# One core, three fused layers: a new order of loads, queries and attention work, and the moves of turned weights on two queues

## The chip, the core and the metric

The kernel runs on one core of one Trainium2 chip. Times are device microseconds (us) of one launch. A core has five engines with a queue of instructions each: TensorE (PE: matmuls and transposes, with its weight loads listed apart as PEld), VectorE (DVE), ScalarE (ACT), GpSimd (POOL) and SyncE (SP), which here only issues DMAs. ACT can issue DMAs too. Every engine works through its own queue in order. Matmuls write to PSUM, which the kernel uses as eight banks of 128 x 512 float32.

The metric is the median of three runs. The profiled execution is another one, with its own time.

## What is computed

Tokens are `x[16, 512, 256]`, all in float32. Three residual layers follow each other:

```python
x = x + 0.5 * slot_ffn(layernorm(x))
x = x + attention(layernorm(x))
x = x + 0.5 * slot_ffn(layernorm(x))

def attention(x):                         # 16 heads of 64, causal, rotary q and k
    q = rope(x @ Wq + bq); k = rope(x @ Wk + bk); v = x @ Wv + bv
    probs = softmax(where(causal, q @ k.T / 8, -inf))
    return (probs @ v) @ Wo + bo

def slot_ffn(x):                          # 16 slots, 16 experts of width 1024, heads of 16
    o = q0 + mha(q0, x, x, d_*)           # slots gather from the tokens
    h = layernorm(o) * g + b              # slot e goes to expert e
    o = o + (silu(h @ W1 + b1) * silu(h @ Wg + bg)) @ W2 + b2
    return mha(x, o, o, c_*)              # tokens read the slots
```

## The kernel before

**Stages.** `ffn(0)`, then `attention`, then `ffn(1)`. An ffn has three parts. `slots_and_experts` loops over the 16 batches i (with two more rounds for the tail): `width(b)` turns a normalized batch so that its width lies on the partitions (8 PE transposes, line 239), `slot_weights` scores the slots (p_ds, line 550), `slot_sums` adds up the tokens (p_z, line 586), `gathered` (p_mo, line 600) projects four batches at a time, `half_of_slots` (p_o, line 340, then its `turned`, p_oT) makes half of the slots ready for the experts. `experts` then goes through 16 experts; each reads three weight tiles of 1 MB that SP loads into twelve buffers, and a buffer is loaded again when its reader is done. `combine` is the third part (p_cs, p_vw, p_catT, p_cy).

**Queries.** The projection of a batch's tokens for `combine`, `queries(b)` (p_cq, line 383, 8 matmuls), can be put anywhere before `combine`. One is called in the slots' loop, two at its end (lines 501 and 503), two after it (lines 514 and 515), and the rest are `fillers` of `experts`: one per expert, and as many of the last experts get one as there are fillers.

**Order.** PE's order is written by hand for the whole kernel. In the slots' loop and in attention the orders of DVE, ACT, POOL and SP are the program's too; elsewhere (the first loads, `combine`) a planner chooses them.

**Attention.** A unit u is one batch and four heads: 64 units. Step u of the loop at line 1101 works on five units at once, as a pipeline:

- `sums(u)`: weights times values (p_av, line 1054, 32 matmuls on 128 rows x 64 columns of the array), and ACT's two writes of oT with the bias;
- of unit u+1 (`old`): the four `turn_most`, `turn_corner` and `turn_rest` (seven DVE transposes of 32 x 32 blocks into the tile sq, line 1001), POOL's scaling of the last quarter of the weights before them, then `move`: sixteen DMAs of 160 KB which carry blocks from 32 partitions q of sq to 32 partitions k of prT (line 1024, all on SP). sq and prT are single tiles. `sums(u+1)` waits for the sixteen;
- of unit u+2 (`new`): `scores` (p_as, line 956: four row tiles of 32 rows side by side) of token tile 3, later of tiles 2, 1 and 0; `exps` (DVE masks and takes the minimum out of PSUM, line 974, ACT takes the exponential, line 978); `scaled` (DVE's reciprocal, line 983, then POOL, line 986);
- of unit u+1: `values` (p_v, line 920, in two halves of 8 matmuls, ACT copies each);
- of unit u+3: queries and keys with rotary (p_q and p_k, line 898; DVE's eight products, line 904, and POOL's four sums, lines 909 and 910). At a new batch (`fresh`, every fourth unit) also `enter` (ACT normalizes), `width` (p_ahT, line 883) and `with_bias` (POOL);
- `leave(u, 0)` and `leave(u, 2)`: the output projection (p_ay, line 1070, 16 matmuls). Its addition to x on DVE (line 1076) is handed back as a function; the next step calls it after `move`.

In PE's order the step is: sums, scores of tile 3, half of the values, queries, keys, the other half of the values, the scores of tiles 2, 1 and 0, leave. Queries, keys, values, leave and `width` use the whole array (128 rows x 128 columns).

PSUM banks are taken in turn: a group takes the bank of the group eight places earlier, and waits until that one has been read. `token_stats` is a batch-norm pair on DVE (lines 198 and 199) that later layer norms need; `spread` and `scales` make the inverse deviations of two batches from them, through a square root on ACT.

**First loads.** SP issues the four pieces of x[0], then d_Wq and d_Wk, then the other x; ACT issues the slot query and three small rows. In `combine` of ffn 0, at j = 0 attention's weights are requested (`ahead[0]`) and at j = 9 `first_pieces` (`ahead[1]`) takes the statistics of batches 0 and 1 in one go (`pair_stats(0)`, 8 pairs) and starts attention.

Of the kernel before, what the change touches and what calls it, by code (L numbers as in the profile page):

```python
# [9 lines left out]
F32 = mybir.dt.float32  # L10
AF = mybir.ActivationFunctionType
ALU = mybir.AluOpType
# [3 lines left out]
P = 128  # L16
# [31 lines left out]
def macaron_kernel(ctx: ExitStack, tc: tile.TileContext, a: dict, out: bass.AP):  # L48
# [47 lines left out]


    with tc.tile_pool(name="setup", bufs=1) as su:
        for t in range(NT):
            nc.sync.dma_start(xs[0][:, t, :], xin[0][:, t, :])  # L100
        sq = su.tile([NS, D], F32, tag="sq", name="sq")
        nc.scalar.dma_start(sq, a["slot_query"][0])
        d_wq = chunks(su.tile([P, NC, D], F32, tag="d_wq", name="d_wq"), a["d_Wq"], nc.sync)
        d_wk = chunks(su.tile([P, NC, D], F32, tag="d_wk", name="d_wk"), a["d_Wk"], nc.sync)
        drow = su.tile([3 * NC, P], F32, tag="drow", name="drow")
        for r, nm in enumerate(("d_bq", "d_bk", "d_bv")):
            nc.scalar.dma_start(drow[r * NC:(r + 1) * NC, :], a[nm].rearrange("(c p) -> c p", p=P))
# [216 lines left out]
    def slots_and_experts(n, ss, load, w, for_slots, hTs, kT, vT):  # L324
# [70 lines left out]
        with tc.tile_pool(name=f"disp{n}", bufs=2) as dp, \  # L395
# [37 lines left out]
            with tc.manual_schedule(engines={mybir.EngineType.DVE, mybir.EngineType.Activation,  # L433
                                             mybir.EngineType.Pool, mybir.EngineType.SP}):
                for i in range(NB + 2):
# [7 lines left out]
                    count(1)  # L443
                    if i < NB:
                        at, scaled = slot_weights(dp, i, hTs[i], lambda: count(1))
                    ahead = i + 2 if i < 2 else i + 1 if i > 2 else NB
                    if ahead < NB:
                        width(ahead)
                    if i - 1 in back:
# [48 lines left out]
                    ahead = i + 3 if i < 1 else i + 2 if i > 1 else NB  # L498
                    if ahead < NB:
                        hs[ahead] = normalized(dp, ahead, 4)  # L500
                queries(order.pop(0))
                gathered(NB // GB - 1, zT, moT, wvm)
                queries(order.pop(0))
                tail = half_of_slots(1)
        gp.close()
        with tc.tile_pool(name=f"late{n}", bufs=1) as lw, \
# [202 lines left out]
    def combine(n, cp, qTs, kT, vT, c_wo, cbo, last, ahead, later):  # L709
# [82 lines left out]
        for j in range(nj + 4):  # L792
            b = j // 2
            if ahead is not None and j == 0:
                ahead[0]()
            if ahead is not None and j == 9:
                pieces = ahead[1]()
            if j < nj:
                weigh(j, kbd)
                if j % 2 == 0:  # L800
                    values(b, vbd)
                    if b + 1 < NB:
                        nxt = of_slots(b + 1)
                    fetch(b + 3)
                else:
                    kbd, vbd = nxt
            if j == 3:
                later()
            if 0 <= j - 3 < nj:
                turned(j - 3)  # L810
            if j >= 4:
                onto_tokens(j - 4)
            if j >= nj - 1:
                for one in pieces[:2]:
                    one()
                del pieces[:2]
# [27 lines left out]
    def attention(qp, wq, wk, wv, wo, cos, sin, row):  # L844
# [87 lines left out]
        class Weights:  # L932
# [82 lines left out]
                self.turn(1, (0, HG), [(1, 2)], 1, (1, 3))  # L1015
                self.turn(1, (0, HG), [], 0, (0,))

            def move(self):


                prT = prTs[self.u] = ap.tile([P, NSQ, HG, blocks * SQ], F32, tag="prT", name=f"prT{self.nm}")
                for k in range(NSQ):
                    for q in range(NSQ):
                        nc.sync.dma_start(prT[k * SQ:(k + 1) * SQ, q, :, :], self.sq[q * SQ:(q + 1) * SQ, k, :, :])

            def turn_at_once(self):

# [37 lines left out]
        def leave(u, t0):  # L1065
            b, hg = units[u]
            py = ps(f"p_ay{b}_{hg}_{t0}")
            for t in range(2):
                for pair in range(HG // 2):
                    nc.tensor.matmul(py[:, t * D:(t + 1) * D], oTs[u][:, pair, (t0 + t) * P:(t0 + t + 1) * P],  # L1070
                                     wo[:, hg * (HG // 2) + pair, :],
                                     start=(pair == 0), stop=(pair == HG // 2 - 1))

            def added():
                xt = xs[b][:, t0:t0 + 2, :]
                nc.vector.tensor_tensor(xt, py.rearrange("p (t d) -> p t d", t=2), xt, ALU.add)
                if hg == NHG - 1:
                    nc.sync.dma_start(xout[b][:, t0:t0 + 2, :], xt)
            return added

# [14 lines left out]
        seen = 2 * NHG  # L1097
        with tc.manual_schedule(engines={mybir.EngineType.DVE, mybir.EngineType.Activation,
                                         mybir.EngineType.Pool, mybir.EngineType.SP}):
            gone = []  # L1100
            for u in range(-2, nu):
                new = ws[u + 2] = Weights(u + 2) if u + 2 < nu else None
                qk = queries_keys(u + 3)
                old = ws.get(u + 1)
                fresh = u + 3 < nu and units[u + 3][1] == 0
                if fresh:
                    enter(units[u + 3][0])
                if u + 2 == nu:
# [6 lines left out]
                if old and u + 2 == nu:  # L1115
                    old.turn_at_once()
                elif old:
                    old.turn_most(0)
                    old.scaled((1, 0), slice(0, HG // 2))
                    old.turn_most(1)  # L1120
                    old.scaled((1, 0), slice(HG // 2, HG))
                    old.turn_most(2)
                    old.turn_most(3)
                    old.turn_corner()
                    old.turn_rest()
                    old.move()
                for one in gone:
                    one()
                if fresh:
                    with_bias(units[u + 3][0])  # L1130
                if u + 4 in stds:
                    scales((u + 4) // (PB * NHG), stds.pop(u + 4))
                if fresh:
                    width(units[u + 3][0])
                if new:
                    new.scores((3,))
                    new.exps((3,))

                for at in range(seen, min(u + 13, NB * NHG)):
                    token_stats(*divmod(at, NHG))  # L1140
                seen = max(seen, u + 13)
                if u >= NHG + 1:
                    token_stats(*divmod(u - NHG - 1, NHG))
                if new:
                    new.scaled((3,))
                if 0 <= u + 1 < nu - 1:
                    values(u + 1, 0)
                for one in qk:
                    one()
                if 0 <= u + 1 < nu - 1:  # L1150
                    values(u + 1, 2)
                if 0 <= u + 5 < nu and (u + 5) % (PB * NHG) == 0:
                    stds[u + 5] = spread((u + 5) // (PB * NHG))
                if new:
                    new.scores((2,))
                    new.scores((1, 0))
                    new.exps((2,))
                    new.exps((1, 0), lambda: new.scaled((2,)))

                if u == nu - NHG:  # L1160
                    for g in range(NB // PB - 1):
                        pair_rstd(g)
                if u == nu - 1:
                    for g in range(PB):
                        entered[g] = xs[g]
                        for t in range(NT):
                            i = (g % PB) * NT + t
                            nc.vector.tensor_scalar(xs[g][:, t, :], xs[g][:, t, :], mvs[g // PB][:, i, 0:1],
                                                    rstds[g // PB][:, i:i + 1], ALU.subtract, ALU.mult)
                gone = [leave(u, 0), leave(u, 2)] if u >= 0 else []  # L1170
                if u >= nu - 2:
                    for one in gone:
                        one()
                    gone = []
            token_stats(NB - 2, NT - 1)
        yield
    with ExitStack() as es:
# [3 lines left out]
            stage.append(attention_weights(es.enter_context(tc.tile_pool(name="attw", bufs=1, side="right"))))  # L1181

        def first_pieces():
            pair_stats(0)
            pair_rstd(0)
            stage.append(attention(es.enter_context(tc.tile_pool(name="attq", bufs=1, side="right")), *stage.pop()))
            return next(stage[0])

# [44 lines left out]
```

## Time and profile before

| What | us |
|---|---|
| median of three runs (2343.24 to 2343.98) | 2343.69 |
| the profiled execution's own time | 2343.35 |
| its span, first to last instruction | 2341.6 |
| PE busy | 2286.4 |
| DVE busy | 1754.4 |
| ACT busy | 1123.7 |
| POOL busy | 1062.1 |

The stages in the span: ffn 0 from 0 to about 417, attention to about 1953, ffn 1 to the end. The granted TensorE clock was 0.992 over the span.

A busy PE says little of how fast it works, since matmuls overlap in the array and their ends are modelled; the start of one group and the start of the next say more. In rows of the timeline the columns are start, duration, engine, line, operation and tiles; the number in brackets is idle time before the row and what ended it. Matmul rows carry the array's rows x columns (128*128, 32*128, 128*64). Rows of DMA-issuing instructions (SPq, ACTq) are not counted as busy.

### The profile page before, as it was taken

How to read it: one execution, taken by the hardware profiler on the slowest of the kernel's cores; microseconds unless marked ns; L12 is line 12 of the kernel's file. 1: busy time of each engine (PE TensorE's matmuls, PEld its weight loads, DVE VectorE, ACT ScalarE, POOL GpSimd, SP SyncE). 2: the span in 40 equal slices, each digit the busy share in tenths (PEclk: the TensorE clock that was granted, in tenths of full speed). 3: DMA queues.
4: the chain of work that ended last, by engine and by line, in shares of the span. 5: the costliest groups of instructions: out<-in, count | busy, mean ns of one | idle time of the engine just before them, and what ended most of it. 6: DMA issues, size and time to landing. Idle time of an engine off the chain costs nothing. (4 is left out here: it accounts for less than half of the span.)

```text
span 2341.6 us, 42264 instructions
## 1 busy us (share of the span) xinstructions
PE 2286.4 (98%) x14496; PEld 1454.2 (62%) x14496; DVE 1754.4 (75%) x4659; ACT 1123.7 (48%) x3047; POOL 1062.1 (45%) x1692
## 2 busy tenths in 40 slices
PE   7999999899999999999999999999999999998999
PEld 5664588465565656565656565656656566664588
DVE  6732388888888888888898888888888865432387
ACT  5742243445455545454545545554555454542233
POOL 2210053565555655555656555556565541210043
PEclk9999999999999999999999999999999999999999
DMA  7839851354545464545555555646464643739834
GB/s 231 242 122 390 330 132 55 67 115 111 125 102 129 103 141 95 132 112 121 114 116 120 120 116 113 130 100 137 91 142 103 130 105 106 238 106 391 341 114 139
DMA packets 159710, 346.77 MB, mean 148 GB/s; under 512 B 38980, under 2 KB 98952, under 8 KB 151304
## 3 DMA queue, kind: packets, MB, share of 16 engines
q1 hardware_dynamic: 158908, 343.53, 55.1%
q8 instruction: 115, 1.88, 0.3%
q14 instruction: 99, 0.81, 0.1%
q10 hardware_dynamic: 588, 0.54, 0.1%
HBM read 148.95 MB, written 29.88 MB: 76 GB/s over the span
## 5 line engine op out<-in xcount | busy, mean ns | idle before, releaser
L986 POOL TENSOR_SCALAR pr<-pr,ars 128x512 f32<-128x512 f32 (+3 forms) x1024 | 522.1, 532 | 631.0 <-DVE ars L983 631.0
L978 ACT ACTIVATE pr<-pr,amn 128x512 f32<-128x512 f32 (+3 forms) x1024 | 560.6, 549 | 268.9 <-DVE amn L974 268.8
L974 DVE CUSTOM_DVE_ANT_0 pr<-p_as,causal 128x512 f32<-128x512 f32 (+3 forms) x1024 | 433.9, 484 | 95.2 <-PE p_as L956 95.2
L1001 DVE STREAM_TRANSPOSE sq<-pr 128x768 f32<-128x768 f32 x441 | 379.0, 906 | 0.8 <-DMA prT<-sq 0.6
L956 PE MATMUL p_as<-k,q 32*128 32x128 f32 (+3 forms) x4096 | 324.8, 444 | 6.6 <-DVE k L904 3.4
L1054 PE MATMUL p_av<-prT,v 128*64 128x512 f32 (+3 forms) x2048 | 291.4, 437 | 3.2 <-DMA prT<-sq 3.2
L956 PEld LDWEIGHTS p_as<-k,q 32*128 32x128 f32 x4096 | 192.1, 186 | 106.7 <-issue 49.6
L920 PEld LDWEIGHTS p_v<-wv,ahT 128*128 128x128 f32 x1024 | 189.3, 190 | 97.4 <-issue 75.7
L920 PE MATMUL p_v<-wv,ahT 128*128 128x256 f32 x1024 | 248.1, 385 | 0.0
L923 ACT COPY v<-p_v 128x512 f32<-128x512 f32 x128 | 73.3, 574 | 352.3 <-PE p_v L920 352.3
L1070 PE MATMUL p_ay<-wo,aoT 128*128 128x256 f32 x1024 | 240.0, 388 | 0.2 <-ACT aoT L1061 0.2
L1054 PEld LDWEIGHTS p_av<-prT,v 128*64 128x64 f32 x2048 | 137.7, 137 | 162.7 <-issue 136.1
L898 PE MATMUL p_k<-ahT,wk 128*128 128x512 f32 x512 | 230.6, 592 | 0.4 <-DVE amn L974 0.4
L898 PE MATMUL p_q<-ahT,wq 128*128 128x512 f32 x512 | 230.5, 592 | 0.2 <-ACT ahT L884 0.2
L1070 PEld LDWEIGHTS p_ay<-wo,aoT 128*128 128x128 f32 x1024 | 190.4, 191 | 31.9 <-ACT aoT L1061 0.6
L978 ACT ACTIVATION_READ_ACCUMULATOR pr<-pr,amn 128x1 f32 x1024 | 191.7, 187 | 0.0
L898 PEld LDWEIGHTS p_k<-ahT,wk 128*128 128x128 f32 x512 | 97.2, 190 | 122.8 <-issue 110.7
L898 PEld LDWEIGHTS p_q<-ahT,wq 128*128 128x128 f32 x512 | 97.1, 190 | 95.8 <-issue 85.4
L719 POOL TENSOR_TENSOR kbd<-kT,own 128x256 f32<-128x256 f32 x32 | 19.7, 618 | 274.7 <-DVE kT L682 240.8
L1061 ACT ACTIVATE aoT<-p_av,bcol 128x512 f32<-128x512 f32 x128 | 87.4, 684 | 108.4 <-PE p_av L1054 108.4
L772 PE MATMUL p_cy<-vw,catT 128*128 128x256 f32 x512 | 121.4, 381 | 2.0 <-ACT catT L764 2.0
L550 PE MATMUL p_ds<-hT,qk 128*128 128x512 f32 x256 | 116.9, 600 | 0.0
(167 smaller groups left out, 3258.5 us busy)
## 6 DMA issues: line engine op xcount, KB each, us to landing
prT<-sq SPq DMA_DIRECT2D x1008, 160.0 KB
w<-in_e_W_dram SPq DMA_DIRECT2D x64, 1024.0 KB
w<-in_e_Wg_dram SPq DMA_DIRECT2D x32, 1024.0 KB
out_dram<-x SPq DMA_DIRECT2D x64, 256.0 KB
awaya<-sqa SPq DMA_DIRECT2D x25, 512.0 KB
atT<-awaya SPq DMA_DIRECT2D x100, 128.0 KB
xl<-in_attn_x_dram SPq DMA_DIRECT2D x16, 512.0 KB
xl<-out_dram SPq DMA_DIRECT2D x16, 512.0 KB
```

The costliest lines, as they stand in the source:

```text
L550: nc.tensor.matmul(psc, qk[:, k, c * P:(c + 1) * P], hT[:, k, :], start=(k == 0), stop=(k == NC - 1))
L772: nc.tensor.matmul(py[:, t * D:(t + 1) * D], atT[:, c, t * P:(t + 1) * P], vws[b][:, c, :], start=(c == 0), stop=(c == NC - 1))
L898: nc.tensor.matmul(pq, self.w[:, k, at:at + P], hTs[self.b][:, k, :], start=(k == 0), stop=(k == NC - 1))
L920: nc.tensor.matmul(pv[:, t * 256:(t + 1) * 256], hTs[b][:, k, (t0 + t) * P:(t0 + t + 1) * P], wv[:, k, hg * HG * DQ:(hg + 1) * HG * DQ], s ...
L956: nc.tensor.matmul(banks[j][:, at:at + w], q[n][j * 32:(j + 1) * 32, i * P:(i + 1) * P], k[n][j * 32:(j + 1) * 32, :w], start=(n == 0), st ...
L974: nc.vector.tensor_tensor_reduce(out=self.at(i, j), in0=banks[j][:, at:at + w], in1=causal[:, S - w:], scale=-1.0 / math.sqrt(DQ), scalar= ...
L978: nc.scalar.activation(self.at(i, j), self.at(i, j), AF.Exp, bias=self.mn[:, i, j:j + 1], scale=-1.0, accum_out=self.rs[:, i, j:j + 1])
L986: nc.gpsimd.tensor_scalar(self.at(i, j), self.at(i, j), self.rs[:, i, j:j + 1], 1.0, ALU.mult, ALU.mult)
L1001: nc.vector.transpose(view(self.sq, j * blocks * SQ + dst[0] * SQ, [(blocks * SQ, nh)] + [(s * SQ, n) for s, (_, n) in zip(dst[1:], of)] + ...
L1054: nc.tensor.matmul(po[j * DQ:(j + 1) * DQ, :].rearrange("d (a f) -> d a f", a=NSQ)[:, :, t * SQ:], vs[u][:, t, head * DQ:(head + 1) * DQ], ...
L1061: nc.scalar.activation(oTs[u][:, pair, :].rearrange("d (i a y) -> d a i y", i=NT, a=NSQ), po.rearrange("d (a i y) -> d a i y", i=NT, a=NSQ ...
L1070: nc.tensor.matmul(py[:, t * D:(t + 1) * D], oTs[u][:, pair, (t0 + t) * P:(t0 + t + 1) * P], wo[:, hg * (HG // 2) + pair, :], start=(pair ...
```

## The change

1. *First loads.* d_Wk goes first on SP, before x[0]; d_Wq moves to ACT's queue.
2. *Slots of ffn 0.* `width` of batch 2 moves from round 0 to round 1, that of batch 3 from round 1 to round 2. In ffn 1 nothing changes there.
3. *Queries.* The two calls at the end of the slots' loop go; their batches become fillers of the experts.
4. *Statistics.* The eight pairs of batches 0 and 1 go to j = 8 to 15 of `combine`, one each, and attention starts at j = 17. `pair_stats(0)` and `pair_rstd(0)` go; `scales` makes the same inverse deviations.
5. *Attention.* PE's order becomes: sums, scores of tile 3, half of the values, (`width`), the other half, queries, keys, leave, the scores of tiles 2, 1 and 0. The addition of `leave` follows at once on DVE. The reciprocal and scaling of tile 3 come after the products of queries and keys.
6. *Moves.* Eight of the sixteen DMAs (k = 0 and 2) are issued by SP, eight (k = 1 and 3) by ACT, between its copies of the two halves of the values. Each queue alternates between its two k, and q starts at k and goes round.

```diff
@@ -96,12 +96,12 @@
     with tc.tile_pool(name="setup", bufs=1) as su:
+        d_wk = chunks(su.tile([P, NC, D], F32, tag="d_wk", name="d_wk"), a["d_Wk"], nc.sync)
         for t in range(NT):
             nc.sync.dma_start(xs[0][:, t, :], xin[0][:, t, :])
         sq = su.tile([NS, D], F32, tag="sq", name="sq")
         nc.scalar.dma_start(sq, a["slot_query"][0])
-        d_wq = chunks(su.tile([P, NC, D], F32, tag="d_wq", name="d_wq"), a["d_Wq"], nc.sync)
-        d_wk = chunks(su.tile([P, NC, D], F32, tag="d_wk", name="d_wk"), a["d_Wk"], nc.sync)
+        d_wq = chunks(su.tile([P, NC, D], F32, tag="d_wq", name="d_wq"), a["d_Wq"], nc.scalar)
         drow = su.tile([3 * NC, P], F32, tag="drow", name="drow")
         for r, nm in enumerate(("d_bq", "d_bk", "d_bv")):
             nc.scalar.dma_start(drow[r * NC:(r + 1) * NC, :], a[nm].rearrange("(c p) -> c p", p=P))
@@ -443,7 +443,7 @@
                     count(1)
                     if i < NB:
                         at, scaled = slot_weights(dp, i, hTs[i], lambda: count(1))
-                    ahead = i + 2 if i < 2 else i + 1 if i > 2 else NB
+                    ahead = i + 1 if i > 2 or n == 0 and i > 0 else i + 2 if i < 2 and n == 1 else NB
                     if ahead < NB:
                         width(ahead)
                     if i - 1 in back:
@@ -498,9 +498,7 @@
                     ahead = i + 3 if i < 1 else i + 2 if i > 1 else NB
                     if ahead < NB:
                         hs[ahead] = normalized(dp, ahead, 4)
-                queries(order.pop(0))
                 gathered(NB // GB - 1, zT, moT, wvm)
-                queries(order.pop(0))
                 tail = half_of_slots(1)
         gp.close()
         with tc.tile_pool(name=f"late{n}", bufs=1) as lw, \
@@ -793,7 +791,9 @@
             b = j // 2
             if ahead is not None and j == 0:
                 ahead[0]()
-            if ahead is not None and j == 9:
+            if ahead is not None and 8 <= j < 8 + PB * NT:
+                token_stats(*divmod(j - 8, NT))
+            if ahead is not None and j == 9 + PB * NT:
                 pieces = ahead[1]()
             if j < nj:
                 weigh(j, kbd)
@@ -1015,13 +1015,17 @@
                 self.turn(1, (0, HG), [(1, 2)], 1, (1, 3))
                 self.turn(1, (0, HG), [], 0, (0,))
-            def move(self):
-                prT = prTs[self.u] = ap.tile([P, NSQ, HG, blocks * SQ], F32, tag="prT", name=f"prT{self.nm}")
-                for k in range(NSQ):
-                    for q in range(NSQ):
-                        nc.sync.dma_start(prT[k * SQ:(k + 1) * SQ, q, :, :], self.sq[q * SQ:(q + 1) * SQ, k, :, :])
+            def move(self, eng, half):
+                if half == 0:
+                    prTs[self.u] = ap.tile([P, NSQ, HG, blocks * SQ], F32, tag="prT", name=f"prT{self.nm}")
+                for n in range(NSQ):
+                    for k in (half, half + 2):
+                        q = (k + n) % NSQ
+                        eng.dma_start(prTs[self.u][k * SQ:(k + 1) * SQ, q, :, :],
+                                      self.sq[q * SQ:(q + 1) * SQ, k, :, :])
             def turn_at_once(self):
@@ -1070,13 +1074,10 @@
                     nc.tensor.matmul(py[:, t * D:(t + 1) * D], oTs[u][:, pair, (t0 + t) * P:(t0 + t + 1) * P],
                                      wo[:, hg * (HG // 2) + pair, :],
                                      start=(pair == 0), stop=(pair == HG // 2 - 1))
-            def added():
-                xt = xs[b][:, t0:t0 + 2, :]
-                nc.vector.tensor_tensor(xt, py.rearrange("p (t d) -> p t d", t=2), xt, ALU.add)
-                if hg == NHG - 1:
-                    nc.sync.dma_start(xout[b][:, t0:t0 + 2, :], xt)
-            return added
+            xt = xs[b][:, t0:t0 + 2, :]
+            nc.vector.tensor_tensor(xt, py.rearrange("p (t d) -> p t d", t=2), xt, ALU.add)
+            if hg == NHG - 1:
+                nc.sync.dma_start(xout[b][:, t0:t0 + 2, :], xt)
@@ -1097,12 +1098,15 @@
         seen = 2 * NHG
         with tc.manual_schedule(engines={mybir.EngineType.DVE, mybir.EngineType.Activation,
                                          mybir.EngineType.Pool, mybir.EngineType.SP}):
-            gone = []
             for u in range(-2, nu):
                 new = ws[u + 2] = Weights(u + 2) if u + 2 < nu else None
                 qk = queries_keys(u + 3)
                 old = ws.get(u + 1)
                 fresh = u + 3 < nu and units[u + 3][1] == 0
+                stats = [divmod(at, NHG) for at in range(seen, min(u + 13, NB * NHG))]
+                seen = max(seen, u + 13)
+                left = [divmod(u - NHG - 1, NHG)] if u >= NHG + 1 else []
                 if fresh:
                     enter(units[u + 3][0])
                 if u + 2 == nu:
@@ -1123,41 +1127,33 @@
                     old.turn_most(3)
                     old.turn_corner()
                     old.turn_rest()
-                    old.move()
-                for one in gone:
+                    old.move(nc.sync, 0)
+                if u + 4 in stds:
+                    scales((u + 4) // (PB * NHG), stds.pop(u + 4))
+                if new:
+                    new.scores((3,))
+                if 0 <= u + 1 < nu - 1:
+                    values(u + 1, 0)
+                if fresh:
+                    width(units[u + 3][0])
+                if old and u + 2 < nu:
+                    old.move(nc.scalar, 1)
+                if 0 <= u + 1 < nu - 1:
+                    values(u + 1, 2)
+                if new:
+                    new.exps((3,))
+                for one in stats:
+                    token_stats(*one)
+                for one in qk:
                     one()
+                if new:
+                    new.scaled((3,))
                 if fresh:
                     with_bias(units[u + 3][0])
-                if u + 4 in stds:
-                    scales((u + 4) // (PB * NHG), stds.pop(u + 4))
-                if fresh:
-                    width(units[u + 3][0])
-                if new:
-                    new.scores((3,))
-                    new.exps((3,))
-                for at in range(seen, min(u + 13, NB * NHG)):
-                    token_stats(*divmod(at, NHG))
-                seen = max(seen, u + 13)
-                if u >= NHG + 1:
-                    token_stats(*divmod(u - NHG - 1, NHG))
-                if new:
-                    new.scaled((3,))
-                if 0 <= u + 1 < nu - 1:
-                    values(u + 1, 0)
-                for one in qk:
-                    one()
-                if 0 <= u + 1 < nu - 1:
-                    values(u + 1, 2)
                 if 0 <= u + 5 < nu and (u + 5) % (PB * NHG) == 0:
                     stds[u + 5] = spread((u + 5) // (PB * NHG))
-                if new:
-                    new.scores((2,))
-                    new.scores((1, 0))
-                    new.exps((2,))
-                    new.exps((1, 0), lambda: new.scaled((2,)))
-                if u == nu - NHG:
+                if u == nu - NHG + 1:
                     for g in range(NB // PB - 1):
                         pair_rstd(g)
                 if u == nu - 1:
@@ -1167,11 +1163,16 @@
                             i = (g % PB) * NT + t
                             nc.vector.tensor_scalar(xs[g][:, t, :], xs[g][:, t, :], mvs[g // PB][:, i, 0:1],
                                                     rstds[g // PB][:, i:i + 1], ALU.subtract, ALU.mult)
-                gone = [leave(u, 0), leave(u, 2)] if u >= 0 else []
-                if u >= nu - 2:
-                    for one in gone:
-                        one()
-                    gone = []
+                if u >= 0:
+                    leave(u, 0)
+                    leave(u, 2)
+                for one in left:
+                    token_stats(*one)
+                if new:
+                    new.scores((2,))
+                    new.scores((1, 0))
+                    new.exps((2,))
+                    new.exps((1, 0), lambda: new.scaled((2,)))
             token_stats(NB - 2, NT - 1)
         yield
     with ExitStack() as es:
@@ -1181,8 +1182,6 @@
             stage.append(attention_weights(es.enter_context(tc.tile_pool(name="attw", bufs=1, side="right"))))
         def first_pieces():
-            pair_stats(0)
-            pair_rstd(0)
             stage.append(attention(es.enter_context(tc.tile_pool(name="attq", bufs=1, side="right")), *stage.pop()))
             return next(stage[0])
```

## The prediction

> **What bounds the kernel.** I read the busy times first, then the busy time by stage, the waits in the middle of attention, one step of attention in the timeline, and then the places where PE stands.
>
> ```profile
> PE 2286.4 (98%) x14496; PEld 1454.2 (62%) x14496; DVE 1754.4 (75%) x4659; ACT 1123.7 (48%) x3047; POOL 1062.1 (45%) x1692
> ```
>
> ```profile
> 600.00:1800.00 1200.00, 1200.00 (x7373) 719.62 (x7372) 1048.91 (x2883) 625.61 (x1911) 695.84 (x1064) 1.00 0.54 117
> 417.00:500.00 83.00, 75.95 (x428) 41.83 (x431) 68.46 (x185) 38.49 (x120) 49.70 (x73) 0.96 0.44 96
> ```
>
> The columns after the window are PE, PEld, DVE, ACT, POOL, the clock, the share of DMA time. In attention PE is busy for 1200.00 of 1200 us at full clock, DVE for 1048.91 (87%). The waits of that stretch have no PE row at all; the largest are followers:
>
> ```profile
> POOL pr L986 <- DVE ars L983: 497.9, 101, 7.4
> ACT v L923 <- PE p_v L920: 283.6, 50, 6.3
> DVE pr L974 <- PE p_as L956: 73.3, 56, 1.7
> ```
>
> So PE's groups set the step, and a group is priced from its start to the next one's start. One step:
>
> ```profile
> 1002.73 4.53 PE L1054 MATMUL p_av<-prT,v 128*64 128x512 f32 x32
> 1007.18 2.00 PE L956 MATMUL p_as<-k,q 32*128 32x512 f32 x16
> 1009.11 1.99 PE L920 MATMUL p_v<-wv,ahT 128*128 128x256 f32 x8
> 1010.94 3.60 PE L898 MATMUL p_q<-ahT,wq 128*128 128x512 f32 x8
> 1014.38 3.60 PE L898 MATMUL p_k<-ahT,wk 128*128 128x512 f32 x8
> 1017.81 1.89 PE L920 MATMUL p_v<-wv,ahT 128*128 128x256 f32 x8
> 1019.63 2.88 PE L956 MATMUL p_as<-k,q 32*128 32x384 f32 x48
> 1022.44 3.72 PE L1070 MATMUL p_ay<-wo,aoT 128*128 128x256 f32 x16
> 1026.09 4.09 PE L1054 MATMUL p_av<-prT,v 128*64 128x512 f32 x26
> ```
>
> It takes 1026.09 - 1002.73 = 23.36 us. The reader is to see that no group waits, and that the array's shape changes four times.
>
> **Attention's order.** Inside a run, 256-wide matmuls start every 0.216 us. p_ay takes 1022.44 to 1026.09 = 3.65 for sixteen, 16 x 0.216 = 3.46: its two edges to other shapes cost 0.19. Among the whole-array groups no edge shows (p_q and p_k take 3.43 each, 8 x 0.429). Put behind p_k, p_ay loses its own two edges; the stretch keeps one at each end. That is 0.19 a step over 62 steps: 12.1. `width` at a new batch takes 1.02 for 8 transposes of 0.109, so joining the stretch saves 0.15, 15 times: 2.3. **Attention: -14.4**, a step of 23.17, if nobody comes late.
>
> Who could? With S the start of sums, PE now ends p_ay at S+20.36 and the last scores at 23.17. DVE's first mask of tile 2 followed its scores by 1.59 before (1019.63 to 1021.22), so it starts at 21.95, and from there to the end of the turns DVE ran 4.32 + 6.54, to which leave's two additions (1.25 together) no longer add, since they come earlier, at 20.5 to 21.7; with the products and the statistics between, I put the turns' end at S + 9.6 of the next step (21.95 + 10.86 = 32.81). In the trace of before it is S+6.06:
>
> ```profile
> 1008.79 26.41 SPq L1024 DMA_DIRECT2D prT<-sq  x21
> ```
>
> The moves then have 13.5 us to the next sums instead of 17.3. From the records of DMA packets, the first of sixteen lands 2.45 after its issue, the others every 0.807, all within 14.45. At that pace sums would wait some 1 us a step. The moves' price is therefore the question of this change.
>
> **The moves.** Sixteen issues of 590 ns stand in a row on one queue:
>
> ```profile
> L1024 SPq DMA_DIRECT2D prT<-sq x1008: 507/590/1912, 441.0 to 1924.1; - x168
> ```
>
> A landing each 0.807 is little more than that. A packet of 5 KB took 402 ns at the median, but 196 in the uncontended tenth. In the old order four DMAs in a row write the same 32 partitions; where k changes, the gap is 0.711. In the diagonal order neither side repeats a quarter, and two queues issue. Ends: 0.807 (nothing won) and 0.40 (two 196 ns packets). The Trainium skill speaks against it: "SBUF — State Buffer", section "Can I just issue two DMAs to hit both halves?", has two concurrent DMAs at partitions 0 and 64 only 6% ahead of one, and "DMA: Bandwidth & Descriptors", section "Issuing engines are not separate DMA queues", has several issuers save only the issue time, usually small beside the DMA. Here it is not small: 0.59 against 0.807. By the rule, an estimate, r = 0.76 us per DMA; by the packet row, 0.40 and up. I take r = 0.5, nearer to the fast packets, because DMAs that differ on both sides are what those packets look like. No row shows it.
>
> Now the wait that this adds. ACT's eight DMAs stand in its queue between its copies of the two halves of v, and need the turns: ACT stands from about S+8.9 to S+9.6, then issues. Behind it wait the second copy of v (0.58) and the four exponentials of tile 3 (2.85); for those waits DVE's reciprocal (line 983), then POOL's scaling (5.46), and on DVE leave's additions and everything after. The reciprocal must come by S+19.75. So 19.75 - 9.6 - 0.58 - 2.85 = 6.7, less 0.2 of semaphores: **ACT may be held 6.5 us** after the turns. A DMA waits for the previous one on its landing semaphore; eight of them are taken in turn by both queues, so in sixteen DMAs each has two, and ACT's last issue comes when about half have landed: 3.05 + 6.5 r with the queues alternating. r = 0.5 gives 6.3 (no loss), 0.66 gives 7.3 (0.8 a step), 0.76 gives 8.0 (1.5 a step, 93 in all), 0.807 gives 8.3 (1.8). If SP's eight take all the semaphores first, ACT's wait for them: 7.5 to 12 us, 1.0 to 5.5 a step. The gain of 0.23 a step is gone at r = 0.57, and the whole change's at about r = 0.6. SP gets nothing else behind the moves but the outputs of that step, which nobody reads.
>
> **Attention's start.** The first sums wait once for the moves:
>
> ```profile
> 455.70 6.15 PE L1054 MATMUL p_av<-prT,v 128*64 128x512 f32 x32 [3.21 <-DMA prT<-sq]
> ```
>
> Faster moves give back up to 3.2; **-2**, at worst 0. The reciprocal and scaling of tile 3 moved behind the products, the joined `stats` and `scales`: DVE's and ACT's, both with spare time (2.6 us of ACT before tile 3's exponentials), 0; if DVE decided they'd cost their own 0.6 a step.
>
> **Slots' tail.** Two `queries` go there, in both ffn:
>
> ```profile
> 161.93 3.60 PE L383 MATMUL p_cq<-hT,c_Wq 128*128 128x512 f32 x8
> 165.46 1.10 PE L600 MATMUL p_mo<-zT,wvm 128*32 128x64 f32 x64
> 166.49 3.70 PE L383 MATMUL p_cq<-hT,c_Wq 128*128 128x512 f32 x8
> ...
> 179.13 3.66 PE L628 MATMUL p_u<-w,hET 128*32 128x256 f32 x64 [0.75 <-DVE hET L365]
> ```
>
> They hid ACT's copy of zT before p_mo (0.8) and that of moT before p_o (0.8). Gone: 2 x 3.45 = 6.9; uncovered: 1.6; the experts start 5.3 earlier. The two become fillers. The experts are set by weights, 3 MB in 7.65 us per expert (PE waits 0.4 of each at p_u), and early experts run from twelve loaded buffers with about 7.6 of slack, so 6.9 of fillers fit and loading follows the readers that free buffers 5.3 earlier. 2 x -5.3 = **-10.6**; between -12 and 0, the latter if loading alone sets the experts' end.
>
> **First loads and slots.** Two stretches:
>
> ```profile
> 8.81 1.12 PE L121 MATMUL p_wkT<-ident,d_wk 128*128 128x128 f32 x4 [4.42 <-DMA d_wk<-in_d_Wk_dram]
> 11.34 1.04 PE L128 MATMUL p_q<-sqT,d_wq 128*128 128x16 f32 x4 [1.41 <-DVE sqT L115]
> ...
> 26.43 2.81 PE L239 MATMUL p_hT<-ident,h 128*128 128x128 f32 x8 [3.46 <-ACT h L231]
> 29.03 5.25 PE L550 MATMUL p_ds<-hT,qk 128*128 128x512 f32 x8
> ```
>
> With `width(2)` a round later, p_ds of batch 1 fills the wait of 3.46 for h of batch 2 instead of following it; it took 5.25 after the pause, at a lower clock, against 3.44 elsewhere. The point that came at 34.11 comes at about 28.5. d_Wk earlier takes from x[0], which is late then by as much as it saves: 0. **-5**, between -2.5 and -6.
>
> **Statistics.** The eight pairs in one lump delay ACT's catT:
>
> ```profile
> 327.94 2.49 PE L772 MATMUL p_cy<-vw,catT 128*128 128x256 f32 x8 [2.01 <-ACT catT L764]
> ```
>
> One a round is hidden by DVE's idle half; attention starts a round later. **-1**, between -2 and +1.
>
> **Sum.** -14.4 - 2 - 10.6 - 5 - 1 = -33.0. The profiled execution's span is 2341.6; 2308.6 after. The median of the runs lies 2.1 above the span (2343.69; the profiled execution's own time is 2343.35): **2311**.
>
> **Rivals.** *ACT late by a part.* r = 0.61 to 0.66, or the semaphores of ACT's half partly behind SP's: 0.4 to 0.85 a step over 62 steps is 25 to 53 back: 2336 to 2364. For it: packets of this size mostly take 400 ns. Against: they then share a quarter of the partitions.
> *ACT's issues decide (the other side).* At the rule's r, or with SP's eight ahead of ACT's, the step grows by 1.5 to 2.8: 2311 + 93 to 174 = 2404 to 2485. Place: ACT held by its DMAs between the two copies of v. It decides from 6.9 us on, r = 0.6. For it: the trace has never had ACT wait for a DMA in the step, and ACT's slack before tile 3's exponentials (2.61) is the largest it shows. Against: the issues of early loads on ACT took 0.24 to 0.52.
> *Attention's gain does not show*, the change does not do what it says: the edges reappear between leave and the scores, or DVE, busy at 87%, sets the step. Then 2311 + 14 = 2325. For it: in every eighth step DVE came 1.4 late and the scores ran 0.62 longer. Against: DVE has 3 us a step to spare.
>
> **How the numbers follow.** Forecast 0.46 (its own range 2302 to 2322, from the start's, tail's and combine's bounds); ACT late by part 0.22; ACT decides 0.18; no attention gain 0.12; more than forecast 0.02. No change is told from a change within about 0.2%, 4.7 us. Faster: 0.46 + 0.12 + 0.02 and a little of the part-late case at r = 0.61: 0.62. The rest of that case lies around the old time: 0.04 within, 0.16 slower, with 0.18: 0.34. The range 2300 to 2380 leaves out the case in which ACT decides.
>
> **What would show it.** p_ay directly behind p_k, 3.46 from start to start, and a step of 23.17; eight issues on SP and eight on ACT, all landed within 10 us of the first; DVE's reciprocal of line 983 not idle for ACT's pr; p_u of the first expert some 10 us before 179.13; p_ds twice in a row before 26. It is wrong if p_av waits for the move, if line 983 waits for ACT, or if p_as of tile 2 waits for a bank.

## The result, and the profile after

The changed kernel takes 2485.82 us (2483.55 to 2488.79, four runs) against 2343.70: a ratio of 1.0607, interval 1.0589 to 1.0626. It is slower by 142 us; the forecast was 2311 and the range ended at 2380. The rival in which ACT's issues decide had 2404 to 2485 and a chance of 0.18.

The profiled execution's span is 2481.9, 140.3 more. By stage, from the timelines of both: attention's first scores come at 408.23 instead of 417.79 (-9.6); from there to the end of attention's last p_ay it is 1689.1 instead of 1535.3 (+153.8); ffn 1 takes 384.6 instead of 388.6 (-4.0). All of the loss is in attention; the other two stages gained.

The busy times of the changed kernel, and its busy time by stage for the middle of attention (columns as before):

```profile
PE 2373.0 (96%) x14496; PEld 1505.3 (61%) x14496; DVE 1751.6 (71%) x4658; ACT 1113.8 (45%) x3046; POOL 1065.8 (43%) x1692
```

```profile
600.00:1800.00 1200.00, 1155.91 (x6693) 693.55 (x6686) 950.12 (x2629) 556.96 (x1728) 634.40 (x965) 0.97 0.44 106
```

The same 1200 us hold 6693 matmuls instead of 7373, and PE is idle for only 44 us of them. PE's busy total grew although its matmuls are the same, so busy time hides part of the loss. A little of that is a slower clock: the stretch was granted 0.97 instead of 1.00, which is worth at most 3% of 1200 us, 36 us (an estimate). How the rest divides was not worked out. The waits between 620 and 1800 us (in total, times, longest) say whom the engines waited for:

```profile
ACT v L923 <- DMA prT<-sq: 432.0, 44, 11.6
DVE ars L983 <- ACT pr L978: 191.7, 95, 5.6
PEld p_as L956 <- DVE x L1078: 70.5, 76, 2.9
```

None of these three rows was there before at this size. The first is ACT held in its DMA issues ahead of the second copy of v: 44 steps, 9.8 us each. The other two are the chain behind it. One step in the timeline, with PE's groups:

```profile
1019.56 4.53 PE L1058 MATMUL p_av<-prT,v 128*64 128x512 f32 x32
...
1025.94 3.72 PE L920 MATMUL p_v<-wv,ahT 128*128 128x256 f32 x16
1029.50 3.60 PE L898 MATMUL p_q<-ahT,wq 128*128 128x512 f32 x8
1032.93 3.60 PE L898 MATMUL p_k<-ahT,wk 128*128 128x512 f32 x8
1036.37 3.62 PE L1074 MATMUL p_ay<-wo,aoT 128*128 128x256 f32 x16
1039.91 1.99 PE L956 MATMUL p_as<-k,q 32*128 32x384 f32 x20
1043.56 2.17 PE L956 MATMUL p_as<-k,q 32*128 32x256 f32 x28 [1.65 <-DVE x L1078]
1045.66 4.53 PE L1058 MATMUL p_av<-prT,v 128*64 128x512 f32 x32
```

The stretch is as forecast: p_v to p_ay with no edge inside, p_ay 3.54 with the one edge at its end. The step is 26.10 all the same, because the scores, after their first 20 matmuls, wait for DVE's addition of leave to free a bank. What DVE waited for is in the step before, in the full timeline:

```profile
1003.26 9.90 ACTq L1027 DMA_DIRECT2D prT<-sq  x8
...
1013.21 0.59 ACT L923 COPY v<-p_v 128x512 f32<-128x512 f32 x1 [9.69 <-DMA prT<-sq]
...
1016.65 0.18 DVE L983 RECIPROCAL ars<-ars 128x4 f32<-128x4 f32 x1 [3.80 <-ACT pr L978]
1016.74 1.26 DVE L1078 TENSOR_TENSOR x<-p_ay,x 128x512 f32<-128x512 f32 x2
```

ACT issues for 9.90 us, then copies v, then takes tile 3's exponentials; DVE's reciprocal waits for them, the additions stand behind the reciprocal, the scores behind the additions, and the next turns behind the scores.

### The profile page after: what moved, and what is told of

The parts are those of the page before. It is cut to its first block, busy times and chain, and to the rows that moved or that the text cites. A ratio compares the mean times of both kernels' runs of the same rounds, so it can differ in the third digit from the quotient of the medians.

```text
span 2481.9 us, 42540 instructions
## 1 busy us (share of the span) xinstructions
PE 2373.0 (96%) x14496; PEld 1505.3 (61%) x14496; DVE 1751.6 (71%) x4658; ACT 1113.8 (45%) x3046; POOL 1065.8 (43%) x1692
## 5 line engine op out<-in xcount | busy, mean ns | idle before, releaser
L956 PE MATMUL p_as<-k,q 32*128 32x128 f32 (+3 forms) x4096 | 401.2, 462 | 69.6 <-DVE x L1078 62.6
L956 PEld LDWEIGHTS p_as<-k,q 32*128 32x128 f32 x4096 | 233.5, 194 | 203.4 <-DVE x L1078 98.7
L1058 PE MATMUL p_av<-prT,v 128*64 128x512 f32 (+3 forms) x2048 | 321.4, 470 | 1.7 <-DVE amn L974 1.7
L909 POOL TENSOR_TENSOR q<-q,q 128x512 f32<-128x512 f32 x64 | 81.3, 1270 | 486.9 <-DVE q L904 486.9
L1058 PEld LDWEIGHTS p_av<-prT,v 128*64 128x64 f32 x2048 | 146.3, 147 | 171.4 <-issue 145.2
L920 PE MATMUL p_v<-wv,ahT 128*128 128x256 f32 x1024 | 241.9, 387 | 0.0
L983 DVE RECIPROCAL ars<-ars 128x4 f32<-128x4 f32 x255 | 42.7, 167 | 274.4 <-ACT pr L978 273.0
L1074 PE MATMUL p_ay<-wo,aoT 128*128 128x256 f32 x1024 | 231.8, 379 | 0.2 <-ACT aoT L1065 0.2
```

Of the source, the lines that this page charges most:

```text
L909: nc.gpsimd.tensor_tensor(self.halves[0], self.m[0, 0], self.m[1, 0], ALU.subtract)
L920: nc.tensor.matmul(pv[:, t * 256:(t + 1) * 256], hTs[b][:, k, (t0 + t) * P:(t0 + t + 1) * P], wv[:, k, hg * HG * DQ:(hg + 1) * HG * DQ], s ...
L956: nc.tensor.matmul(banks[j][:, at:at + w], q[n][j * 32:(j + 1) * 32, i * P:(i + 1) * P], k[n][j * 32:(j + 1) * 32, :w], start=(n == 0), st ...
L1058: nc.tensor.matmul(po[j * DQ:(j + 1) * DQ, :].rearrange("d (a f) -> d a f", a=NSQ)[:, :, t * SQ:], vs[u][:, t, head * DQ:(head + 1) * DQ], ...
```

## The experiments

Two words first: ACT's *hold* is the time in a step from its first issue (or first added copy) to its second copy of v, and the *pitch* of the moves is the time from one landing to the next.

Theory A: ACT is held by its issues, and once the hold is long enough the step is the hold plus a constant. Theory B: the new order itself sets the step. Theory C: two queues make the transfers late, and ACT's standing costs nothing by itself. No kernel leaves work out; two add some.

**All moves on SP, diagonal order.**

```diff
-                    old.move(nc.scalar, 1)
+                    old.move(nc.sync, 1)
```

> The changed kernel with all sixteen moves on SP, still in diagonal order. Theory A (ACT is held by its eight issues, 9.84 us a step, and that sets the step at 26.09): with no issue on ACT the step falls to PE's own, a mean of 23.4 to 23.6, and the time to 2314 to 2330, if the moves keep their 0.71 us each (all landed 13.1 us after the first issue). Theory B (the new order itself sets it: the additions of leave at once on DVE keep banks from the scores, whoever issues the moves): step 25.5 or more, 2450 to 2486. Between: if it was the second queue and not the order of pairs that brought 0.80 down to 0.71, the sums wait about 1 us a step and the time is 2375 to 2395.

Measured: 2307.35 us, ratio to the kernel before 0.9850 (0.9833 to 0.9866), 178 us less than the changed kernel. The timeline of its PE:

```profile
1008.96 4.53 PE L1058 MATMUL p_av<-prT,v 128*64 128x512 f32 x32
...
1029.32 2.88 PE L956 MATMUL p_as<-k,q 32*128 32x384 f32 x48
1032.12 4.53 PE L1058 MATMUL p_av<-prT,v 128*64 128x512 f32 x32
```

No wait, and 23.16 a step: the forecast's 23.17. The time is 7 us under the lowest that was expected. In the median the pitch is 0.668 us, and all sixteen have landed 12.65 after the first issue. Theory B falls: everything of the new order is in this kernel. And the second queue was not what shortened the pitch; one queue has a shorter one.

**All moves on SP, rows as before.**

```diff
-                for n in range(NSQ):
-                    for k in (half, half + 2):
-                        q = (k + n) % NSQ
+                for k in (2 * half, 2 * half + 1):
+                    for q in range(NSQ):
 ...
-                    old.move(nc.scalar, 1)
+                    old.move(nc.sync, 1)
```

> The changed kernel with all sixteen moves on SP in the order of the kernel before (k outside, q inside). Theory A: ACT is free; the moves land every 0.80 us, 14.5 after the first issue, about 1 us too late for a window of 13.5, so the sums wait for them: a mean step of 24.2 to 24.7, 2360 to 2395. If the order of pairs is worth nothing, it equals the run with SP in diagonal order. Theory B: 2450 to 2486.

Measured: 2349.82, ratio 1.0029 (1.0017 to 1.0041). The pitch is 0.801, all land in 14.49, and sums wait:

```profile
1000.75 4.53 PE L1057 MATMUL p_av<-prT,v 128*64 128x512 f32 x32 [1.55 <-DMA prT<-sq]
```

The mean of 53 steps is 24.10 (23.42 in diagonal order), and both it and the time are under what was expected, 24.2 and 2360. Every other step is long (24.1 to 25.0); those between take as long as without a wait, 23.2, or 24.0 where a new batch begins. A step that waited leaves the next moves that much more time. The window of 13.5 us that the prediction worked out is real: in diagonal order the next sums start 13.45 after the first issue, so 14.49 does not fit and 12.65 does.

**ACT's half behind its exponentials.**

```diff
-                if old and u + 2 < nu:
-                    old.move(nc.scalar, 1)
 ...
                 if new:
                     new.exps((3,))
+                if old and u + 2 < nu:
+                    old.move(nc.scalar, 1)
```

> The changed kernel with ACT's eight moves put behind its exponentials of tile 3 instead of between its copies of the two halves of v; still two queues and diagonal order. Theory A: the second copy, the exponentials, DVE's reciprocal and what follows no longer wait; ACT's issues then run from about S+13.2, SP's eight are in flight before them, and all have landed about S+23: mean step 23.4 to 24.0, 2314 to 2350. Theory B: 2450 to 2486.

Measured: 2331.93, ratio 0.9956 (0.9947 to 0.9966). The same two queues and the same order of pairs, 154 us less than the changed kernel: it is what stands behind the issues that costs. It doesn't reach 2307. Many ordinary steps take 23.17, others 24 to 26, and one row of the waits points to the reason:

```profile
ACT pr L978 <- DMA prT<-sq: 89.9, 10, 9.0
```

In ten steps of the stretch it is ACT's own issues that end last before its exponentials of the next tiles. The hold moved to another place, where it mostly fits. (The trace is of the longest of 14 executions, 2342.26.)

**Work in place of the issues: a hold without a second queue.** Two kernels, with 18 and 30 copies:

```diff
-                    old.move(nc.scalar, 1)
+                    old.move(nc.sync, 1)
+                    held = ap.tile([P, 256], F32, tag="held", name=f"held{u}")
+                    for _ in range(18):
+                        nc.scalar.copy(held, old.sq[:, 0, :, :].rearrange("p h f -> p (h f)")[:, 0:256])
```

> All moves on SP in diagonal order (2307.35 us), and in the place of ACT's eight issues 18 copies on ACT of 128x256 from the turned weights to a tile that nobody reads: added work that holds ACT for about 6 to 6.5 us after the turns, with no second queue. Theory A (held ACT; the step is the hold plus 16.25 us as soon as that is more than 23.2, which the changed kernel's 26.09 - 9.84 gives): under the point of 6.9, so no loss to speak of, 2307 to 2325. Theory C (what was lost came from two queues sharing the transfers, not from ACT standing): 2307 to 2310.

> The same with 30 copies, about 10 us of hold. Theory A: a step of about 26.2 with the sums' start paced by ACT, 2450 to 2500, with the same waits as the changed kernel: DVE's reciprocal on ACT's exponentials, the scores of tile 2 on DVE's addition. Theory C: 2307 to 2315, since DVE's and PE's queues hold nothing new.

Measured: 2347.94 (ratio 1.0017, 1.0009 to 1.0024) and 2771.02 (1.1820, 1.1802 to 1.1838). The copies were longer than expected, 0.43 us each. The timelines of ACT, 18 copies first:

```profile
1007.25 7.82 ACT L1143 COPY held<-sq 128x256 f32<-128x256 f32 x18 [0.71 <-DVE sq L1001]
1014.99 0.58 ACT L923 COPY v<-p_v 128x512 f32<-128x512 f32 x1
```

```profile
1014.03 13.07 ACT L1143 COPY held<-sq 128x256 f32<-128x256 f32 x30
1027.01 0.58 ACT L923 COPY v<-p_v 128x512 f32<-128x512 f32 x1
```

Holds of 7.74 and 12.98 us, steps of 23.87 and 30.64, with moves that land every 0.67 as without a hold. So theory C falls. Both times were outside the numbers expected for theory A, since the hold was, but the relation holds for the first: 23.87 - 7.74 = 16.1, the changed kernel's 26.10 - 9.89 = 16.2. A second queue adds nothing to it. At 12.98 it is 17.7; there the granted clock of the stretch is 0.90, and the 28 scores behind the wait take 2.87 and 3.52 us in two steps that the timeline shows, 2.17 in the changed kernel. How much of the 1.5 that explains was not tried.

**Four issues on ACT instead of eight.**

```diff
-                    old.move(nc.scalar, 1)
+                    old.move(nc.scalar, 1, (0, 1))
+                    old.move(nc.sync, 1, (2, 3))
```

> The changed kernel with four of ACT's eight moves handed to SP (SP twelve, ACT four, the same place in ACT's order, diagonal). Theory A (the step is ACT's hold after the turns plus 16.1 us, or PE's 23.17): the hold falls from 9.84 to 4 to 6.5 us, under 7.05, and the step to PE's own: 2305 to 2325. If any issue on ACT behind the turns costs its share (half of the DMAs, half of the loss): 2395.

Measured: 2318.54, ratio 0.9890 (0.9875 to 0.9905). The hold is 5.98 and the ordinary step 23.18, though half the issues are still there: a short hold costs little, not its share. Of the 11 us that this kernel takes longer than the one with all moves on SP, the last step but one makes 7.5 (32.02 instead of 24.55). Together:

| Run | hold of ACT, us | step, us | step - hold |
|---|---|---|---|
| all on SP, diagonal | none | 23.17 | |
| four issues | 5.98 | 23.18 | |
| 18 copies | 7.74 | 23.87 | 16.1 |
| the change, eight issues | 9.89 | 26.10 | 16.2 |
| 30 copies | 12.98 | 30.64 | 17.7 |

(Medians over 53 steps.) The point from which the hold decides is 23.17 - 16.1, about 7.05.

**Two queues, rows as before.**

```diff
-                for n in range(NSQ):
-                    for k in (half, half + 2):
-                        q = (k + n) % NSQ
+                for k in (half, half + 2):
+                    for q in range(NSQ):
```

> The changed kernel with its two queues, but each half in the order of the kernel before (k outside, q inside; SP k = 0 and 1, ACT k = 2 and 3). If two queues take from a move what diagonal order gives, the pitch is 0.78 to 0.82, ACT is held about 11 us and the step is about 27.2: 2540 to 2570. If two queues with different k help by themselves (SP and ACT write different quarters at any time), the pitch is 0.66 to 0.72 and the time that of the changed kernel, 2470 to 2500.

Measured: 2491.36, ratio 1.0626 (1.0611 to 1.0642). The pitch is 0.784, but the hold is 9.81 and the step 26.18, as with diagonal order. Neither expectation came true: the pitch is the slow one and the time that of the fast one. The hold does not follow the pitch. Every DMA of the trace reports its landing on one of eight semaphores, which both queues share. In the step above, from 1003.26 on, ACT's third, fourth and sixth issues each start 0.02 us after one of SP's moves has landed, the one before on the same semaphore (1006.77, 1008.99 and 1011.30). ACT waits for SP's transfers, which are in flight for 3.5 to 4.7 us in that step. Of the 124 gaps of over 0.1 us between ACT's issues in 53 steps of the changed kernel, 105 end so, and they make 3.2 us of the hold in the mean; 6.0 are the eight issues themselves. That this cross-wait lengthens the hold is read from the records; a kernel with landing semaphores of its own for ACT was not tried.

**Parts 1 to 4 alone, and with diagonal moves.** The kernel before with the first loads, the widths, the queries and the statistics of the change (hunks 1 to 4 of the diff, and that of `first_pieces`); then with this as well:

```diff
-                for k in range(NSQ):
-                    for q in range(NSQ):
+                for half, n, k in [(h, n, k) for h in range(2) for n in range(NSQ) for k in (h, h + 2)]:
+                    for q in ((k + n) % NSQ,):
```

> The kernel before with parts 1 to 4 of the change alone (first loads, width in ffn 0, queries as fillers, statistics one a round); attention as before. From the trace of the changed kernel: attention's first scores 9.6 us earlier, ffn 1 about 4 us shorter, so -13.5: 2330 (2326 to 2334). By the steps of the prediction -16.6: 2327. If what is won ahead of attention were taken back by it: 2340.

> Parts 1 to 4 of the change (2331.45 us) and the moves in diagonal order, all on SP; attention's order as before. The moves land 0.67 instead of 0.80 us apart, but in this order they already land 2.8 us before the sums, so only the first sums, which wait once, come earlier: 2329 to 2332. If faster moves help in any other way (less traffic in the way of other engines' reads): below 2327.

Measured: 2331.45 (ratio 0.9952, 0.9937 to 0.9967) and 2328.55 (0.9935, 0.9919 to 0.9952). With the two SP kernels above, all four with parts 1 to 4, this is a square:

| | moves in rows | diagonal |
|---|---|---|
| attention's order as before | 2331.45 | 2328.55 |
| attention's order changed | 2349.82 | 2307.35 |

The order alone loses 18, the faster moves alone gain 3 (hardly more than the spread of the runs), both together gain 24. The order is worth something only with the faster moves.

**Single parts.** Queries alone (hunk 3) and statistics alone (hunk 4 and `first_pieces`) on the kernel before, and the widths taken back in the best kernel:

> The kernel before with part 3 alone (two queries in each ffn become fillers of the experts). The prediction's step gave 2 x -5.3 = -10.6. From the traces ffn 1, in which nothing else changed, lasts 4.0 less, though its experts start 5.7 earlier: 2 x -4.0 = -8.0, 2334 to 2338. If the loads of the weights alone set the experts' end, 2343.

> The kernel before with part 4 alone (the eight pairs of statistics one a round). The prediction's step gave -1. From the two traces, combine of ffn 0 up to attention's first keys and queries lasts 113.5 before and 108.5 after: 5.0 less, half of it PE's idle time of 2.0 and the catch-up, half the lower pace of PE behind that pause. So 2336 to 2340 if attention keeps it; 2342 to 2344 if only -1 or attention takes it back.

> All moves on SP in diagonal order, with the widths of batches 2 and 3 back where they were (the first loads stay changed). The prediction's step gave -5 to loads and widths together. If the widths were worth it: 2312. If, as the trace of the changed kernel reads, the second copy of batch 2's turned width is now uncovered (PE stands 2.29 us and p_ds then runs at a low clock, 6.69 us), so that nothing is left of the gain: 2306 to 2309.

Measured: queries 2332.84 (ratio 0.9953, 0.9938 to 0.9968), -10.7 against the 2343.56 measured beside it; statistics 2340.43 (0.9986, 0.9980 to 0.9993), -3.1; old widths 2304.70 (0.9834, 0.9819 to 0.9848), 2.7 under the kernel with the new ones, whose own runs overlap it at the edge. It is the fastest of all. The widths of the change are worth nothing, rather less. The start of ffn 0 in the changed kernel:

```profile
20.03 7.03 PE L548 MATMUL p_ds<-hT,qk 128*128 128x512 f32 x16
...
30.26 0.98 PE L571 MATMUL p_atT<-ident,at 128*128 128x128 f32 x7 [0.77 <-POOL at L561]
33.54 6.69 PE L548 MATMUL p_ds<-hT,qk 128*128 128x512 f32 x8 [2.29 <-ACT hT L241]
```

The wait for h is filled, as forecast. Then p_ds of batch 2 comes right behind its own width and waits 2.29 for ACT's copy hT; and behind the pause it takes 6.69 instead of 3.60. Batch 3's p_ds starts at 45.32 instead of 43.73, and with the old widths, but the new first loads, at 45.05. The first loads gained nothing either: p_ds of batch 0 starts at 19.07 to 21.12 in the eleven profiles that have them, and at 18.63 to 19.55 in the three that do not.

The statistics gave more than their pause of 2.01. Before, behind it, the groups ran slower for a while:

```profile
330.22 1.91 PE L741 MATMUL p_cs<-kbd,cq 128*128 128x128 f32 x8
331.93 1.42 PE L730 MATMUL p_vw<-c_wo,vbd 128*128 128x256 f32 x4
...
335.35 1.05 PE L741 MATMUL p_cs<-kbd,cq 128*128 128x128 f32 x8
```

## Why the prediction was wrong

- *Attention's order* (a step of 23.17 "if nobody comes late"): right, 23.16 in the kernel with all moves on SP. Its gain was larger than 14.4: 24 us between that kernel and parts 1 to 4 alone, 21 where those have diagonal moves too, since the longer steps of every eighth unit (23.99) went too, which the sum had at 0, and the last step but one fell from 29.95 to 24.55.
- *The window and the place of the hold*: right. "ACT may be held 6.5 us", and "it decides from 6.9 us on"; it is about 7.05. The chain (copy, exponentials, line 983, additions) is the one that the changed kernel shows.
- *"I take r = 0.5"*: wrong. Two queues in diagonal order land a move every 0.708, against 0.807 assumed for before and 0.76 by the page's rule. The fast packets of 196 ns, 8% of the moves' packets before, were no sign of what diagonal order gives: the median went from 402 to 347 only (304 with one queue). Nor was the gap of 0.711 "where k changes": it stands at the second of three such places alone, the other two have 0.807 and 0.808 (medians over 53 steps).
- *"3.05 + 6.5 r with the queues alternating"*: the step that failed. With r = 0.708 it gives 7.65, a loss of 1.15 a step or some 70 us; measured was a hold of 9.9 and 2.9 a step. The hold is no function of the pitch: 9.89 at 0.708, 9.81 at 0.784. The formula took the queues to alternate, so that ACT's last issue comes when half of the moves have landed. The eighth landing does come when it says, 7.8 after ACT's first issue. But by then SP has issued all its eight (7.7), and ACT, which waits about twice a step for a landing of SP's, is done only at 9.8, when ten have landed. The prediction had this as its other case (7.5 to 12 us, 1.0 to 5.5 a step), gave it too little, and priced it as a rival with 2.8 a step at most: that end, 2485, is the result.
- *Queries* -10.6: -10.7 measured, but not as 2 x -5.3. In the profile of that kernel attention's first scores come 9.5 earlier and ffn 1 is 3.3 shorter, so that the sum fits so well is in part luck; why the two differ was not pursued. *Statistics* -1: -3.1 measured; what was left out is that PE runs slower behind the pause. *First loads and slots* -5: nothing gained. The step "p_ds of batch 1 fills the wait" holds, but what is late next, the copy of hT, was not named. *Attention's start* -2: from first scores to first sums 36.55 instead of 37.91, -1.4.

The forecast of 2311 would have been near for the changed kernel with one word changed, `nc.scalar` to `nc.sync`: 2307.35. That is partly luck too: attention gave some 8 us more than the sum had, the first loads and slots 5 less.

## What to carry to other kernels

A DMA issue is an instruction in its engine's queue, and it can stand there for as long as transfers of another queue take to land: before one is put on a compute engine, list what is queued behind it and by when that must be done. Price such a hold by its own waits, not by the pace of the transfers. Faster transfers and a tighter order can each be worth little or less alone and good together, so try the four combinations before a part is dropped.

## What the runs showed of the hardware

- The order of pairs sets the pace at the same bytes. The same sixteen moves of 160 KB on the same queue land every 0.801 us when four in a row write the same 32 partitions, and every 0.668 when a move (but for one of the sixteen) shares neither its source's nor its target's 32 partitions with the one before: near the 0.635 at which SP issues them.
- A second issuing queue gave almost nothing: 0.801 to 0.784 in rows, and 0.668 to 0.708, a loss, in diagonal order (why was not tried). "DMA: Bandwidth & Descriptors", section "Issuing engines are not separate DMA queues", of the Trainium skill says that issuing from several engines saves only the issue time; these runs agree, and show the price that it leaves out, the engine's own time (9.9 us of ACT for eight issues of 0.6).
- Behind a pause of PE of about 2 us the next groups were slower, by about as much again: p_ds took 6.69 instead of 3.60 behind 2.29 of idle time (in the records the granted clock is 0.5 from 32.8 to 39.6 us), and before, behind 2.01, p_cs took 1.91 instead of 1.05 (0.5 from 329.3 to 332.7). In attention the granted clock fell with PE's waits, from 1.00 to 0.97, and to 0.90 with the longest hold.
